# Attention scores of two heads issued in turns, with a third score tile in PSUM

## The chip, the core and the metric

The kernel runs on one core of a Trainium2 chip. Five engines work from instruction streams of their own: TensorE (PE, with its weight loads shown as PEld), VectorE (DVE), ScalarE (ACT), GpSimd (POOL) and SyncE (SP, which issues the DMAs here). Matrix products land in PSUM, which on each of 128 partitions has eight banks of 512 fp32 values. The metric is the time of one execution on the device in microseconds (us), the median of several runs.

## The reference

Input x is (4, 512, 512), batch by time by channel, and cond is (4, 512). Four layers follow each other, each added to its input:

```
x = x + attention(x, cond)        # RMS norm scaled and shifted from cond, 16 heads of 32 channels,
                                  # q and k RMS-normed, softmax over all 512 keys, o + o @ W_out
x = x + GRU(x), state0 = cond     # 512 steps in time, one after the other:
                                  #   r, z = sigmoid(x W_ih + b_ih + h W_hh + b_hh)   (two thirds of the columns)
                                  #   n = tanh(i_n + r * h_n);  h = (1 - z) * n + z * h
x = x + conv4(x, taps of cond)    # causal, over time, by channel
x = x + conv4(x, taps of cond) + b
```

All is fp32. The kernel writes most matrices as a sum of two f16 parts (hi and lo) and makes three products of them.

## The kernel before

**The two kinds of work.** The GRU is a chain of 512 steps, none of which can start before the one ahead of it. Everything else (attention of later rows, the gate inputs x W_ih, the two convolutions, the output) is background work, cut into blocks of 32 time steps: block i holds rows 32i to 32i+31 of all four batches, 128 rows in all. Block i must have its gate inputs in DRAM (`GD[i]`) before step 32i.

**The prologue** (up to step 0) makes keys (`KH`, `KL`) and values (`V`) for all of x, then the attention of block 0 and the first heads of block 1 by `q_.flush`, then the gate inputs of block 0 (`tail`).

**One step** of the loop (`for t in range(T)`) issues in this order:

- `q_.head`: background stages on DVE, ACT and POOL, within budgets `DVE_B`, `ACT_B`, `POOL_B` per step;
- 64 products into `X` (r and z) and `Y` (n) at line 1227: 16 with `A` (needed first), 48 with `BT`;
- DVE transposes `X` into `TX` (line 1241), adds into `S`; ACT makes the gates `ZT` by tanh; ACT fills `X` for the next step from `G` (`seedX`); DVE transposes `Y` into `TY` (1253), a scan forms `N` (1254); ACT takes its tanh into `D` (1255) and fills `Y` for the next step (`seedY`, line 1124);
- `q_.pe`: background products on PE, chunks whose declared costs add up to at most `PE_SLOT` = 1600 ns (`SLOT0` = 2000 for the first 40 steps); I call this the step's slot;
- `keep_warm`: a product of zeros where the slot's products had under 384 columns; it goes into an `m` tile, or into the unused part of `Y`'s bank (`idle`) where both `m` tiles are taken;
- two DVE scans give `A` and `HS`, the new state (1264, 1265), and `prep` makes `BT` and `HH` of them (1130 to 1132).

Every engine takes its instructions in this order, so background work delays the chain only where an engine has not finished it when the chain's next instruction could start.

**The background queue** (`Queue`) is a planner that runs while the program is written. A task has products in chunks, each with a declared cost, then stages on other engines, in later steps. It takes buffers by name when it starts: `m` (two PSUM tiles for transposes, projections and gate inputs), `s` (two PSUM tiles for scores), `P` (four SBUF tiles for the exponentials `PX`), `PT` (four for their transposes), `O` (one PSUM tile for the attention output). Tasks are tried in order of a priority. If a block is not ready when its gate inputs are due, `q_.flush` issues all that it still needs at once.

**One head of attention** is three tasks: `S` (scores: three chunks of four products of 32 rows of q and k, one per batch, into four bands of 32 partitions of one `ps` tile, line 439; then DVE's maximum `mx` at line 446, POOL's `nb`, ACT's exponential `PX` at line 455), `TP` (four transposes of `PX`, line 301, and a copy `PT`) and `AV` (four chunks of four products with V, line 483). Head 4j+q has its 32 channels on partitions 32q to 32q+31 of q and k.

```
for b in range(B):
    nc.tensor.matmul(t[32 * b:32 * b + 32, :], s[x_][R_, j, 32 * b:32 * b + 32], k_[R_, j, b, :],
                     start=(u == 0), stop=(u == 2), skip_group_check=True)
```

PSUM's eight banks: `X`, `N`, `Y`, two `m`, two `s`, one `O`.

Of the kernel before, what the change touches and what calls it, by code (L numbers as in the profile page):

```python
# [8 lines left out]
F32 = mybir.dt.float32  # L9
# [7 lines left out]
P = 128  # L17
# [2 lines left out]
WS = 256.0  # L20
IWS = 1.0 / WS
KS_SCALE = 32.0
PE_SLOT = 1600
SC_ = 215
SLOT0, NS0 = 2000, 40
OFF2 = 120
WARM = 384
GI_T = 2
# [4 lines left out]
          TX=(130, 0), LK=(159, 1.1), S=(4, 4.8), TP=(52, 4.7), AV=(115, 2.6))  # L33
PR1 = dict(PR, ON=(305, 0), TO=(-313, 0), WO=(-28, 0), GI=(-131, 0),
           LK=(128, 0.3), S=(67, 5.1), TP=(100, 6.1), AV=(-432, 6.6))
COLS = {SC_: 192, 680: 256, 137: 64, 150: 128, 330: 128, 140: 256, 111: 256, 123: 256}
DVE_B, ACT_B, POOL_B = 1130, 1900, 3300


# [18 lines left out]
class Queue:  # L58
# [7 lines left out]
    def add(self, tasks):  # L66
        self.pending = sorted(self.pending + list(tasks), key=lambda t: t.prio)
# [60 lines left out]
    def pe(self, budget):  # L128
# [3 lines left out]
        for t in self.pending:  # L132
# [4 lines left out]
            while t.ci < len(t.chunks) and t.chunks[t.ci][0] <= left:  # L137
                c, fn = t.chunks[t.ci]
                fn()
                left -= c  # L140
                self.cols += COLS.get(c, 512)
                t.ci += 1
# [20 lines left out]
def body(ctx, tc, x, cond, W_emb, b_emb, g_norm, W_qkv, g_q, g_k, W_out, W_ih, W_hh, b_ih, b_hh, L3_b, out):  # L163
    nc = tc.nc
# [4 lines left out]
    pg = ctx.enter_context(tc.tile_pool(name="pg", bufs=1, space=PS))  # L169
    pb = ctx.enter_context(tc.tile_pool(name="pb", bufs=1, space=PS))  # L170

    X = pg.tile([P, 256], F32, name="X")
    NN = pg.tile([P, 16, 4], F32, name="N")
    Yb = pg.tile([P, 512], F32, name="Y")
    Y, idle = Yb[:, 0:128], Yb[:, 128:512]

    def pm(name):
        return pb.tile([P, 512], F32, name=name, tag="m", bufs=2)
# [47 lines left out]
    zz = cst.tile([P, 512], F16, name="zz")  # L226
# [12 lines left out]
        for _ in range(n):  # L239
            nc.tensor.matmul(X, zz[:, 0:128], zz[:, 0:256], start=True, stop=True, skip_group_check=True)  # L240

    def keep_warm(n, to=None):

        for _ in range(n):
            nc.tensor.matmul(idle if to is None else to, zz[:, 0:128], zz[:, 0:384], start=to is not None, stop=True, skip_group_check=True)

    nc.tensor.matmul(Yb, zz[:, 0:128], zz, start=True, stop=True, skip_group_check=True)
    clear()
# [50 lines left out]
    def transpose4(dst, src, js=range(4)):  # L299
        for j in js:  # L300
            nc.tensor.transpose(dst[:, 128 * j:128 * j + 128], src[:, 128 * j:128 * j + 128], ident)  # L301
# [14 lines left out]

    X1, XN_, XT_ = {}, {}, {}
    last = dict(S=[], TP=[], R=[])
    q_ = Queue(dict(m=2, s=2, O=1, P=4, PT=4, xb=3, xhl=1, QS=3, q=1, o=1, gi=1, x1=3, L=3))

    def block_tasks(i):
        first, pre_q = i == 0, i < 2
        tl = []
        s = {}

        def add(name, h=0, **k):
            pr = (PR0, PR1)[i] if i < 2 else PR
            p, dp = pr[name[:2] if name[:2] in pr else name[0]]
            t = Task(name, prio=100 * i + p + dp * h + (OFF2 if i == 2 and p < 0 else 0), **k)
            tl.append(t)  # L330
            return t
# [83 lines left out]
        if pre_q:  # L415
            R = Task(f"R{i}")
# [3 lines left out]
        else:  # L420
            R = add(f"R{i}", deps=[Q], acq=["m", "L"], chunks=[(330, rch)], stages=[[("DVE", 410, rs0), ("Pool", 4800, lambda: None)]], rel=["m", "q"], settle=2)
# [4 lines left out]
        STask = {}  # L426
# [2 lines left out]
        prev_av = None  # L429

        def sch(j, q, u):
            def f():
                if u == 0:
                    s[("s", j, q)] = pb.tile([P, 512], F32, name="ps", tag="s", bufs=2)
                t = s[("s", j, q)]
                R_ = slice(32 * q, 32 * q + 32)
                x_, k_ = (("qh", KH), ("qh", KL), ("ql", KH))[u]
                for b in range(B):
                    nc.tensor.matmul(t[32 * b:32 * b + 32, :], s[x_][R_, j, 32 * b:32 * b + 32], k_[R_, j, b, :],  # L439
                                     start=(u == 0), stop=(u == 2), skip_group_check=True)  # L440
            return f

        def smax(j, q):
            def f():
                h = 4 * j + q
                nc.vector.tensor_reduce(s["mx"][:, h:h + 1], s[("s", j, q)], AX.X, ALU.max)  # L446
                (nc.vector if first else nc.gpsimd).tensor_tensor(s["nb"][:, h:h + 1], s["mx"][:, h:h + 1], s["nrq"][:, h:h + 1], ALU.mult)  # L447
            return f
# [10 lines left out]
        def tpch(h, ps=False):  # L459
            def piece(j):  # L460
                def f():
                    if j == 0:
                        s[("pt", h)] = pb.tile([P, 512], F32, name="ptp", tag="s" if ps else "m", bufs=2)
                    transpose4(s[("pt", h)], s["PX"][h], (j,))
                return f
            return [(150, piece(j)) for j in range(4)]
# [21 lines left out]
        for j in range(4):  # L488
            for q in range(4):
                h = 4 * j + q  # L490
                STask[h] = add(f"S{i}.{h}", h, deps=[R], acq=["s", "P"], after=last["S"], chunks=[(SC_, sch(j, q, u)) for u in range(3)],
                               stages=[[("DVE", 600, smax(j, q)), ("Pool", 150, lambda: None)], [("ACT", 720, sexp(j, q))]],
                               rel=["s"], settle=int(first))
                last["S"] = [STask[h]]
                TPs[h] = add(f"TP{i}.{h}", h, deps=[STask[h]], after=last["TP"], acq=["m", "PT"], chunks=tpch(h),
                             stages=[[("ACT", 490, tps(h))]], rel=["m", "P"], settle=int(first))
                last["TP"] = [TPs[h]]
                dep = [TPs[h]] + ([prev_av] if prev_av else [])
                AVs[h] = add(f"AV{i}.{h}", h, deps=dep, chunks=[(137, avch(h, kt)) for kt in range(4)],
                             acq=["O"] if h == 0 else [], rel=["PT"])  # L500
                prev_av = AVs[h]
# [100 lines left out]
        def tail(nx, ahead):  # L602
# [8 lines left out]
            o = s["o"] = at("o", [P, D])  # L611
# [31 lines left out]
            pg = {}  # L643

            def gik(k):
                for n in "rzn":
                    if k == 0:
                        pg[n] = pm("pgn") if n == "n" else pb.tile([P, 512], F32, name="pgi" + n, tag="s", bufs=2)
                    for m, (xa, wi) in enumerate(((xh, 0), (xl, 0), (xh, 1))):
                        nc.tensor.matmul(pg[n], xa[:, k, :], WR[n][:, wi, k, :], start=(k == 0 and m == 0), stop=(k == 3 and m == 2))  # L650

# [21 lines left out]
            for g, n in enumerate("rzn"):  # L673
                gs[n] = at("gs" + n, [P, 4, P], tag=("gs", "PT", "o")[g], bufs=(1, 4, 1)[g])
                o, v = gs[n].rearrange("p q (j s) -> p q j s", j=4), pg[n].rearrange(pj, j=4, q=4)
# [16 lines left out]


    bts = [block_tasks(0), block_tasks(1)]
    need = {i: bts[i]["tasks"] for i in range(2)}

    with ExitStack() as pre_ctx:
# [77 lines left out]
        YS, PY, XN, XHL = {}, {}, {}, {}  # L775
# [3 lines left out]
            nc.scalar.activation(YS[i], XS[i], AF.Copy, scale=RS[:, i:i + 1])  # L779

        def x_t(i, tag=None):
            PY[i] = pb.tile([P, 512], F32, name="py", tag=tag, bufs=2 if tag == "s" else 1) if tag else pm("py")
            transpose4(PY[i], YS[i])

        def x_n(i, e):
# [133 lines left out]
        KV4 = {}  # L919

        def proj(v, kt, b):
            p = pb.tile([P, 512], F32, name="pkv", tag="s", bufs=2)
            XH, XL = XHL[kt]
            n = 0
            for k in range(4):
                for (xa, wi) in ((XH, 0), (XL, 0), (XH, 1)):
                    nc.tensor.matmul(p, xa[:, k, b, :], WKV[:, wi, k, v, :], start=(n == 0), stop=(n == 11))
                    n += 1
            return p
# [87 lines left out]
        for i in range(2):  # L1017
            u, g0 = bts[i], 4 + 4 * i
# [23 lines left out]
        for g in range(33):  # L1042
            p = proj(*ORDER[g]) if g < 32 else None
# [8 lines left out]
            if g < 32:  # L1052
                v, kt, b = ORDER[g]
# [18 lines left out]
    x2b = [lt(f"x2b{i}", [P, 16, 38]) for i in range(2)]  # L1072
    VC, VU, VM = lt("VC", [P, 4, 7]), lt("VU", [P, 4, 4]), lt("VM", [P, 4, 4])
    with tc.manual_schedule(engines={ENG.PE, ENG.DVE, ENG.Activation, ENG.Pool, ENG.SP}):
        ahead = [t for t in need[1] if t.name in ("S1.0", "S1.1", "S1.2")]
        late = [t for t in need[1] if t.name == "S1.3"]
        need[1] = [t for t in need[1] if t not in ahead + late]
        q_.add(need[0] + ahead)
        q_.flush(need[0] + ahead, 1700, lambda used: keep_warm(max(0, int((1050 - used) / 160))), {8: scan_constants})
        gs0 = bts[0]["tail"](bts[1], late)  # L1080
    for i in range(1, NB):
        if i > 1:
# [13 lines left out]
    f = lambda a: a.rearrange("p a k -> p (a k)")  # L1096
# [103 lines left out]
    with tc.manual_schedule(engines={ENG.PE, ENG.DVE, ENG.Activation, ENG.Pool, ENG.SP}):  # L1200
# [3 lines left out]
        for t in range(T):  # L1204
            i = t // 32
# [36 lines left out]
            S = wk.tile([P, 64], F32, name="S", tag="S", bufs=1)[:, 0:32]  # L1242
# [10 lines left out]
            nc.vector.transpose(TY.rearrange("p h j b k -> p j h k b"), Y.rearrange("p (j h k b) -> p j h k b", j=4, h=2, k=4))  # L1253
            nc.vector.tensor_tensor_scan(f(NN), f(zt[:, 0]), TY[:, 0].rearrange("p j b k -> p (j b k)"), 0.0, ALU.mult, ALU.add)  # L1254
            nc.scalar.activation(D1[:, :, 0], NN[:, :, 3], AF.Tanh, scale=0.5 * IWS)  # L1255
            nc.vector.scalar_tensor_tensor(D1[:, :, 1], zt[:, 1, :, 2], 1.0, HH, ALU.add, ALU.mult)
            if 1 < t + 1 < T:
                seedY(t + 1)
            if t == 0:
                seed_first(1, 0)  # L1260
                seed_first(1, 1)
            q_.pe(SLOT0 if t < NS0 else PE_SLOT)
            keep_warm(-(-(WARM - q_.cols) // 384), pm("warm")[:, 0:384] if q_.free["m"] else None)
            nc.vector.tensor_tensor_scan(f(An), f(d0), f(D1), 0.0, ALU.mult, ALU.add)  # L1264
            nc.vector.tensor_tensor_scan(f(HSn), f(d0), f(D1), 0.0, ALU.mult, ALU.add)  # L1265
            A, HS = An, HSn
# [32 lines left out]
```

## Time and profile before

| | us |
|---|---|
| median of 3 runs (lowest, highest) | 1883.12 (1876.41, 1889.18) |
| the profiled execution | 1878.9 |
| its span, first to last instruction | 1876.8 |
| first scan `A` (step 0) ends at | 243.6 |
| steps 0 to 31 end, and what 31 of them take | 350.6, 107.0 |
| steps 32 to 63 end, and take | 458.1, 107.5 |
| steps 64 to 447 end, and take | 1663.2, 1205.1 (3.138 a step) |
| steps 448 to 479 end, and take | 1760.9, 97.7 |
| steps 480 to 511 end, and take | 1857.5, 96.6 (3.018 a step) |

PE is busy for 88% of the span, DVE for 72%, ACT for 65% and POOL for 25%. Times in the profile are from the span's start. A line of a group or a timeline names the engine, the source line, the operation and output<-inputs; "idle before" is the time that its engine waited just before it, with what ended the wait, and "issue" stands where the profile shows nothing that was waited for. Matrix products are pipelined: of a row of several, starts tell more than durations. The share of busy time is a mean over the whole span; the limits differ by stage, so the stages are read one by one.

### The profile page before, as it was taken

Reading aid. Unit: us, or ns where it says so; the run is one execution under the profiler, and the core shown is the slowest. Engines: PE = TensorE matmul, PEld = TensorE weight load, DVE = VectorE, ACT = ScalarE, POOL = GpSimd, SP = SyncE. Lnnn points to the kernel's source line nnn. Section 1 sums busy time; section 2 is a strip of 40 time slices with the busy share of each in tenths; the row PEclk is TensorE's granted clock in tenths of the full one; section 3 lists DMA queues with packets and bytes.
Section 4 is the critical chain, followed back from the end, with each engine's and each line's share of the span. In section 5 each row is a group of like instructions: output and inputs, shape, how many; then the busy total and the mean of one; then the engine's idle time right before and its main releaser. Section 6 shows DMA issues by size and latency. Waiting matters only on the chain.

```text
span 1876.8 us, 114013 instructions
## 1 busy us (share of the span) xinstructions
PE 1655.3 (88%) x48969; PEld 1173.1 (63%) x48969; DVE 1344.8 (72%) x4948; ACT 1220.1 (65%) x4685; POOL 468.6 (25%) x1496
## 2 busy tenths in 40 slices
PE   5788889999999999999999999999999998987553
PEld 2443557667676767676767666676667676765442
DVE  4784467786778777877777777878777877776664
ACT  4542466776767776767676767676676767665543
POOL 1366001222213131222222131313131222121112
PEclk9998899999999999999999999999999999999998
DMA  5652020101010102010101010010101010101000
GB/s 184 226 191 91 25 68 18 50 18 34 18 35 13 39 16 60 13 39 13 40 12 34 19 49 25 19 35 13 39 13 40 13 34 12 35 13 34 11 17 10
DMA packets 68921, 78.11 MB, mean 42 GB/s; under 512 B 6560, under 2 KB 54720, under 8 KB 67776
## 3 DMA queue, kind: packets, MB, share of 16 engines
q1 hardware_dynamic: 68416, 70.82, 12.5%
q8 instruction: 385, 6.31, 1.4%
q14 instruction: 120, 0.98, 0.2%
HBM read 44.58 MB, written 26.21 MB: 38 GB/s over the span
## 4 chain that ended last, share of the span: by engine, by line
PE 47%; DVE 24%; ACT 10%; DMA 8%; issue 6%; SPq 3%; POOL 2%; DVEq 0%; ACTq 0%; POOLq 0%
PE X L1227 21%; PE ps L439 6%; DVE TX L1241 5%; PE Y L1227 5%; PE pgi L568 5%; DMA G<-GD 5%; DVE TY L1253 4%; PE ptp L301 4%; DVE N L1254 4%; ACT D L1255 3%; DVE A L1264 2%; PE po L483 2%; ACT X L1121 2%; SPq L1093 2%; ACT Y L1124 1%
## 5 line engine op out<-in xcount | busy, mean ns | idle before, releaser
L1227 PEld LDWEIGHTS <-BT 128*8 128x8 f16 (+1 forms) x24576 | 450.2, 88 | 82.5 <-issue 19.1
L1227 PE MATMUL X<-Wlo,A 128*4 128x256 f16 x8192 | 313.1, 272 | 126.4 <-DVE A L1264 88.9
L1269 POOL TENSOR_TENSOR x2b<-x,HS 128x16 f32<-128x16 f32 x512 | 126.8, 248 | 1130.7 <-DVE HS L1265 1129.4
L1244 ACT ACTIVATE ZT<-S 128x32 f32<-128x32 f32 x512 | 134.9, 264 | 415.8 <-DVE S L1243 415.3
L1241 DVE STREAM_TRANSPOSE TX<-X 128x256 f32<-128x256 f32 x512 | 229.2, 448 | 210.0 <-PE X L1227 208.9
L1227 PE MATMUL X<-Whi,BT 128*8 128x256 f16 x8192 | 316.0, 273 | 2.7 <-issue 2.4
L1227 PEld LDWEIGHTS <-A 128*4 128x4 f16 x8192 | 151.4, 82 | 219.1 <-DVE A L1264 192.4
L1253 DVE STREAM_TRANSPOSE TY<-Y 128x128 f32<-128x128 f32 x512 | 205.2, 401 | 11.1 <-PE Y L1227 5.0
L1227 PE MATMUL Y<-Whi,BT 128*16 128x128 f16 x8192 | 209.2, 219 | 4.3 <-issue 4.0
L1227 PE MATMUL Y<-Wlo,BT 128*16 128x128 f16 x8192 | 207.9, 219 | 4.2 <-issue 3.7
L1121 ACT ACTIVATE X<-G 128x256 f32<-128x256 f32 x510 | 202.4, 397 | 1.1 <-DMA G<-GD 0.9
L455 ACT ACTIVATE PX<-ps,nb,rqs 128x512 f32<-128x512 f32 x256 | 195.1, 762 | 8.7 <-POOL nb L447 4.8
L1254 DVE TENSOR_TENSOR_SCAN N<-ZT,TY 128x64 f32<-128x64 f32 x512 | 153.3, 299 | 54.9 <-ACT ZT L1244 1.9
L446 DVE TENSOR_REDUCE mx<-ps 128x1 f32<-128x512 f32 x256 | 174.8, 683 | 16.0 <-PE ps L439 15.9
L1264 DVE TENSOR_TENSOR_SCAN A<-D,D 128x32 f16<-128x32 f32 x512 | 115.2, 225 | 94.2 <-ACT D L1255 91.5
L301 PE MATMUL ptp<-ident,PX 128*128 128x128 f32 x1024 | 173.3, 290 | 1.0 <-ACT gs L576 0.6
L1131 ACT ACTIVATE BT<-A 128x64 f16<-128x64 f16 x512 | 131.2, 256 | 52.8 <-DVE A L1264 4.6
L301 PEld LDWEIGHTS ptp<-ident,PX 128*128 128x128 f32 x1024 | 111.4, 143 | 81.7 <-issue 43.1
L475 ACT ACTIVATE PT<-ptp 128x512 f32<-128x512 f32 x248 | 143.3, 582 | 15.7 <-PE ptp L301 15.7
L1124 ACT ACTIVATE Y<-G 128x128 f32<-128x128 f32 x510 | 141.6, 278 | 1.0 <-DMA G<-GD 0.5
L483 PEld LDWEIGHTS po<-V,PT 128*32 128x32 f32 x8192 | 99.1, 112 | 62.5 <-issue 53.8
L483 PE MATMUL po<-V,PT 128*32 128x32 f32 x8192 | 131.1, 200 | 7.3 <-issue 6.5
(266 smaller groups left out, 2818.7 us busy)
## 6 DMA issues: line engine op xcount, KB each, us to landing
GD<-gs SPq DMA_DIRECT2D x45, 256.0 KB
G<-GD SPq DMA_DIRECT2D x512, 16.0 KB
G<-GD SPq DMA_DIRECT2D x512, 8.0 KB
xp<-in_x_dram SPq DMA_DIRECT2D x16, 256.0 KB
xb<-in_x_dram SPq DMA_DIRECT2D x16, 256.0 KB
xhl<-XD SPq DMA_DIRECT2D x32, 128.0 KB
out_dram<-ob SPq DMA_DIRECT2D x16, 256.0 KB
wst<-in_L_cond_W_qkv_dram SPq DMA_DIRECT2D x6, 512.0 KB
```

The source lines that it names most:

```text
L301: nc.tensor.transpose(dst[:, 128 * j:128 * j + 128], src[:, 128 * j:128 * j + 128], ident)
L446: nc.vector.tensor_reduce(s["mx"][:, h:h + 1], s[("s", j, q)], AX.X, ALU.max)
L455: nc.scalar.activation(pe_, s[("s", j, q)], AF.Exp, bias=s["nb"][:, h:h + 1], scale=s["rqs"][:, h:h + 1], accum_out=s["ls"][:, h:h + 1])
L475: nc.scalar.activation(pt_, s[("pt", h)], AF.Copy)
L483: nc.tensor.matmul(s["po"][32 * b:32 * b + 32, 32 * h:32 * h + 32], s["PT"][h][:, kt, 32 * b:32 * b + 32], V[:, 4 * b + kt, 32 * h:32 * h ...
L1121: nc.scalar.activation(X.rearrange("p (g c) -> p g c", g=2), G[(t // 4) % 2][:, t % 4, 0:2, :], AF.Copy)
L1124: nc.scalar.activation(Y, G[(t // 4) % 2][:, t % 4, 2, :], AF.Copy)
L1227: nc.tensor.matmul(dst[32 * qq:32 * qq + M, :], lhs, W[:, k, cols].rearrange("p g (j q s) -> p q g j s", j=4, q=4)[:, qq], start=False, st ...
L1241: nc.vector.transpose(TX.rearrange("p a r -> p (a r)"), X)
L1253: nc.vector.transpose(TY.rearrange("p h j b k -> p j h k b"), Y.rearrange("p (j h k b) -> p j h k b", j=4, h=2, k=4))
L1254: nc.vector.tensor_tensor_scan(f(NN), f(zt[:, 0]), TY[:, 0].rearrange("p j b k -> p (j b k)"), 0.0, ALU.mult, ALU.add)
L1264: nc.vector.tensor_tensor_scan(f(An), f(d0), f(D1), 0.0, ALU.mult, ALU.add)
```

## The change

Three things are changed together, with the constants that go with them:

- `N` no longer has a bank of its own: it takes 64 columns of `Y`'s bank that the products don't write. The bank that comes free is a third `s` tile.
- The scores of two heads with neighbouring partitions are one task, `SP`: each of its three chunks issues eight products, those of the two heads in turns, into two `ps` tiles. `SP` takes two `s` and two `P` at once and counts as done one step later (`settle=1`). Each head's `S` task keeps the maximum and the exponential. A chunk is declared at 225 ns for eight products (before: 215 ns for four).
- `keep_warm` is left out of a step in which both `m` tiles are taken. In the prologue its products go into `idle` as before.

`PE_SLOT` goes from 1600 to 1550 and `SLOT0` from 2000 to 1900.

```diff
-PE_SLOT = 1600
-SC_ = 215
-SLOT0, NS0 = 2000, 40
+PE_SLOT = 1550
+SC_ = 225
+SLOT0, NS0 = 1900, 40
...
-COLS = {SC_: 192, 680: 256, 137: 64, 150: 128, 330: 128, 140: 256, 111: 256, 123: 256}
+COLS = {SC_: 384, 680: 256, 137: 64, 150: 128, 330: 128, 140: 256, 111: 256, 123: 256}
...
-    NN = pg.tile([P, 16, 4], F32, name="N")
     Yb = pg.tile([P, 512], F32, name="Y")
-    Y, idle = Yb[:, 0:128], Yb[:, 128:512]
+    Y, NN = Yb[:, 0:128], Yb[:, 128:192].rearrange("p (a k) -> p a k", k=4)
+    idle = Yb[:, 128:512]
...
-    def keep_warm(n, to=None):
+    def keep_warm(n, to):
         for _ in range(n):
-            nc.tensor.matmul(idle if to is None else to, zz[:, 0:128], zz[:, 0:384], start=to is not None, stop=True, skip_group_check=True)
+            nc.tensor.matmul(to, zz[:, 0:128], zz[:, 0:384], start=True, stop=True, skip_group_check=True)
...
-    q_ = Queue(dict(m=2, s=2, O=1, P=4, PT=4, xb=3, xhl=1, QS=3, q=1, o=1, gi=1, x1=3, L=3))
+    q_ = Queue(dict(m=2, s=3, O=1, P=4, PT=4, xb=3, xhl=1, QS=3, q=1, o=1, gi=1, x1=3, L=3))
...
         def sch(j, q, u):
             def f():
                 if u == 0:
-                    s[("s", j, q)] = pb.tile([P, 512], F32, name="ps", tag="s", bufs=2)
-                t = s[("s", j, q)]
-                R_ = slice(32 * q, 32 * q + 32)
+                    for r in (q, q + 1):
+                        s[("s", j, r)] = pb.tile([P, 512], F32, name="ps", tag="s", bufs=3)
                 x_, k_ = (("qh", KH), ("qh", KL), ("ql", KH))[u]
                 for b in range(B):
-                    nc.tensor.matmul(t[32 * b:32 * b + 32, :], s[x_][R_, j, 32 * b:32 * b + 32], k_[R_, j, b, :],
-                                     start=(u == 0), stop=(u == 2), skip_group_check=True)
+                    for r in (q, q + 1):
+                        R_ = slice(32 * r, 32 * r + 32)
+                        nc.tensor.matmul(s[("s", j, r)][32 * b:32 * b + 32, :], s[x_][R_, j, 32 * b:32 * b + 32], k_[R_, j, b, :],
+                                         start=(u == 0), stop=(u == 2), skip_group_check=True)
...
-                STask[h] = add(f"S{i}.{h}", h, deps=[R], acq=["s", "P"], after=last["S"], chunks=[(SC_, sch(j, q, u)) for u in range(3)],
+                if q % 2 == 0:
+                    SP = add(f"SP{i}.{h}", h, deps=[R], acq=["s", "s", "P", "P"], after=last["S"], chunks=[(SC_, sch(j, q, u)) for u in range(3)], settle=1)
+                    last["S"] = [SP]
+                STask[h] = add(f"S{i}.{h}", h, deps=[SP],
                                stages=[[("DVE", 600, smax(j, q)), ("Pool", 150, lambda: None)], [("ACT", 720, sexp(j, q))]],
                                rel=["s"], settle=int(first))
-                last["S"] = [STask[h]]
...
-        ahead = [t for t in need[1] if t.name in ("S1.0", "S1.1", "S1.2")]
+        ahead = [t for t in need[1] if t.name in ("SP1.0", "S1.0", "S1.1", "SP1.2", "S1.2")]
...
-            keep_warm(-(-(WARM - q_.cols) // 384), pm("warm")[:, 0:384] if q_.free["m"] else None)
+            if q_.free["m"]:
+                keep_warm(-(-(WARM - q_.cols) // 384), pm("warm")[:, 0:384])
```

The other lines of the diff give the score tiles' tag three buffers wherever it is used.

More of the change, by code (lines that the diff above doesn't have):

```diff
@@ L462, in f @@
                     if j == 0:
-                        s[("pt", h)] = pb.tile([P, 512], F32, name="ptp", tag="s" if ps else "m", bufs=2)
+                        s[("pt", h)] = pb.tile([P, 512], F32, name="ptp", tag="s" if ps else "m", bufs=3 if ps else 2)
                     transpose4(s[("pt", h)], s["PX"][h], (j,))
@@ L647, in gik @@
                     if k == 0:
-                        pg[n] = pm("pgn") if n == "n" else pb.tile([P, 512], F32, name="pgi" + n, tag="s", bufs=2)
+                        pg[n] = pm("pgn") if n == "n" else pb.tile([P, 512], F32, name="pgi" + n, tag="s", bufs=3)
                     for m, (xa, wi) in enumerate(((xh, 0), (xl, 0), (xh, 1))):
@@ L781, in x_t @@
         def x_t(i, tag=None):
-            PY[i] = pb.tile([P, 512], F32, name="py", tag=tag, bufs=2 if tag == "s" else 1) if tag else pm("py")
+            PY[i] = pb.tile([P, 512], F32, name="py", tag=tag, bufs=3 if tag == "s" else 1) if tag else pm("py")
             transpose4(PY[i], YS[i])
@@ L921, in proj @@
         def proj(v, kt, b):
-            p = pb.tile([P, 512], F32, name="pkv", tag="s", bufs=2)
+            p = pb.tile([P, 512], F32, name="pkv", tag="s", bufs=3)
             XH, XL = XHL[kt]
@@ L1078, in body @@
         q_.add(need[0] + ahead)
-        q_.flush(need[0] + ahead, 1700, lambda used: keep_warm(max(0, int((1050 - used) / 160))), {8: scan_constants})
+        q_.flush(need[0] + ahead, 1700, lambda used: keep_warm(max(0, int((1050 - used) / 160)), idle), {8: scan_constants})
         gs0 = bts[0]["tail"](bts[1], late)
```

## The prediction

> **What bounds the kernel now.** I read the windows by stage first, because the page's 88% for PE is a mean over unlike stages. Columns: stretch, its length, then busy time and number of instructions of PE, PEld, DVE, ACT, POOL, then the granted clock, the DMA share and GB/s.
>
> ```profile
> 248.30:293.70 45.40, 41.61 (x1430) 30.12 (x1430) 31.23 (x116) 33.55 (x128) 5.30 (x24) 1.00 0.19 53
> 446.20:455.00 8.80, 8.76 (x244) 6.85 (x241) 3.07 (x11) 4.31 (x13) 0.44 (x2) 1.00 0.17 46
> 455.00:1663.20 1208.20, 1138.29 (x36478) 828.23 (x36477) 918.77 (x3527) 863.70 (x3441) 292.05 (x1049) 1.00 0.10 27
> 1237.60:1274.20 36.60, 35.28 (x1257) 24.92 (x1257) 28.53 (x108) 29.20 (x114) 6.57 (x26) 1.00 0.06 16
> 1760.90:1857.50 96.60, 56.68 (x2083) 40.41 (x2083) 63.08 (x269) 47.51 (x229) 18.50 (x57) 1.00 0.05 12
> 176.00:226.00 50.00, 45.23 (x898) 25.93 (x897) 24.70 (x54) 24.35 (x56) 7.23 (x28) 0.80 0.27 107
> ```
>
> The last 32 steps have no attention, and take 96.6/32 = 3.018 us each: that is the bare chain, a floor that cheaper scores don't touch. Against it the stages of the table lose 107.0 - 31 x 3.018 = 13.4 us (steps 0 to 31), 10.9 (32 to 63), 46.2 (64 to 447) and 1.1 (448 to 479): 71.6 us, of which a cheaper slot can win only what PE causes. With PE waiting for `A`, a step's first product starts 0.055 us after the scan. Summed over the steps, the starts are later than that by 9.7 us in steps 1 to 31, 7.5 in 32 to 63 (5.6 of them in one step, the second window) and 6.3 in 64 to 447: PE overruns cost 23.5 us, the rest is late DVE and ACT, and one more thing, read from the waits of PE (waited for: us, times, longest), a timeline row and the DMA queues:
>
> ```profile
> PE X L1227 <- DVE A L1264: 88.9, 140, 1.3
> PE Y L1227 <- issue: 7.7, 17, 1.1
> PE po L483 <- issue: 6.5, 9, 1.7
> ...
> 256.94 0.27 PE L1227 MATMUL Y<-Wlo,BT 128*16 128x128 f16 x5 [1.12 <-issue]
> ...
> q8 instruction: 385, 6.31, 1.4%
> ```
>
> PE stops amid `Y`'s products for 1.12 us with nothing to wait for. PE and PEld have 98,533 records, or 256 for each of the 385 packets of the instruction queue; numbering the records, all 35 such stops inside `X`, `Y` and `AV` lie at the same place of 256. So PE ran out of instructions. After a stop the next packet starts 1.05 to 1.7 us later, and the stop that needs it ends 2.2 to 2.8 us after that: some 3.7 us for 256 instructions, 69 a us, or 209 in a step of 3.02 us. The fourth window is the densest twelve steps: 2,514/36.6 = 68.7 a us.
>
> **Do eight products in turns cost what four do?** The trace has it where one head's last chunk meets the next head's first, which lies on other partitions:
>
> ```profile
> 199.32 0.40 PE L439 MATMUL ps<-KH,ql 32*32 32x512 f16 x4
> 199.33 0.39 PE L439 MATMUL ps<-KH,qh 32*32 32x512 f16 x4
> 199.56 0.38 PE L439 MATMUL ps<-KL,qh 32*32 32x512 f16 x4
> 199.77 0.38 PE L439 MATMUL ps<-KH,ql 32*32 32x512 f16 x4
> ```
>
> Two groups of four start 0.01 us apart, the next 0.23 later; chunks of one head are 0.21 apart. So a pair's chunk costs about 0.22 us, not 0.43, and a pair of heads three of them, 0.65 in place of 1.29.
>
> **The sum, part by part.**
>
> 1. The flush at step 62. It issued 8.6 us of declared work at once, and the step took 8.89 us. The changed program, whose order I read, has block 2 ready before: **-5.8**.
> 2. Other overruns in steps 1 to 63: 9.7 + 7.5 - 5.6 = 11.6, of which 2.3 are two instruction stops inside slots. Declared slots fall from 1,665 to 1,501 ns on average in steps 1 to 31; slots of gate inputs hold 15 products and not 16 (0.12 us less of 0.25 late), every second one of the early slots loses its scores (0.65), the flush at step 30 shrinks from 3.00 to 2.72 us. I leave 3.8 us standing: **-5.5** (-8 to -2).
> 3. Steps 64 to 447: of 6.3 us, 2.1 lie in steps where DVE is late anyway (a maximum, 0.68, and two taps, 0.39 each, before `TX`), 2.4 are stops; the rest goes: **-1.8**. Number and pairs of DVE and ACT stages hardly change (a maximum with taps in one step: 43 times, then 41), so what DVE and ACT cost stays, within 4 us either way.
> 4. The prologue, 20 heads of scores: -20 x 0.325 = -6.5; but its filling rule sees cheaper steps and issues 34 products of zeros for 12, 22 x 0.16 = +3.5; one more planner's step, +1; scores of head 3 of block 1 are ready ahead of the tail (PE 0.65 and part of a wait), -1.1: **-3.1**, between -9 (PE bound everywhere) and +5 (none of it PE's: here ACT's exponential, 0.97 with its accumulator, is on the chain in turns with PE).
> 5. The work ends some 13 steps sooner, so the loss of steps 448 to 479 goes: **-1.0**.
> 6. Products of zeros into `Y`'s bank waited for `seedY` at steps 16 and 417, and made each next step 0.16 late: **-0.3**. With both `m` taken nothing replaces them; the bare-chain stage keeps clock 1.00 with as little on PE.
> 7. `N` in `Y`'s bank. The built order shows one new wait: `seedY` now waits for the tanh that reads `N`, on ACT itself. Rows of ACT before:
>
> ```profile
> 901.14 0.18 ACT L1255 ACTIVATE D<-N 128x16 f32<-128x16 f32 x1
> 901.22 0.28 ACT L1124 ACTIVATE Y<-G 128x128 f32<-128x128 f32 x1
> 901.65 0.26 ACT L1131 ACTIVATE BT<-A 128x64 f16<-128x64 f16 x1 [0.15 <-DVE A L1264]
> ```
>
> `seedY` starts 0.08 after the tanh; waiting, it starts at the tanh's end plus 0.03 (the gap of `D` behind `ZT` at the last step), 0.14 later, and ends at 901.64. Behind it on ACT is `BT` at 901.65, then `HH` and the exponentials; PE needs `BT` only after 16 products of `X`, 0.44 us: **0** (0 to +0.14 x 510 = 71, a rival below). No row excludes it below zero by more than noise, and nothing is saved.
>
> 8. Instruction supply. The number of PE's instructions stays (98,530 before, 98,644 after, by the built programs), but slots with cheap scores hold more of them: of steps 64 to 447, 90 issue over 205 before (in ones and twos), 177 after (mean 226, in runs of 8 to 12). I count what exceeds 209 a step, with a stock of 50 carried over, chosen because before it then gives 11.5 us where the trace has some 12: after, 21.2. With 212 a step the difference is 6.5, with 217 it is 1.6. **+7** (0 to +18).
>
> [...]
>
> Sum: -5.8 - 5.5 - 1.8 - 3.1 - 1.0 - 0.3 + 0 + 7 = -10.5. From the profiled execution's own 1878.9 that is **1868 us**. The median of the runs lies 4.2 above that execution; on it the same change would read 1872.6. One per cent, 18.8 us, is about what a measurement of this kernel can tell from no change.
>
> [...] The rows: granted clock 0.80 in the prologue's attention (last window), 1.00 in every stage of the loop. [...]
>
> **Rivals.**
>
> - *The stops don't grow, and the prologue is bound by PE.* Then part 8 is 0 and part 4 is -6.5 or more: -21, **1858**. For it: overruns shrink, so a stop inside a slot finds room. Against: the densest stretches already run at 69 a us. 0.26.
> - *Instruction supply becomes the bound* (slower). Its place is the runs of dense steps; without a stock, 226/69 = 3.28 us a step where such steps now take some 3.08 with their late DVE: 0.2 x 177 = +35, less 17.5, **1897**. It decides from 0.1 us a dense step, where the gains are used up. 0.14.
> - *`seedY`'s wait reaches the chain*: 0.05 to 0.14 a step, **1885 to 1930**. It decides if `BT` or `X`'s 17th product starts later after `A`. 0.05.
> - *The change doesn't do what it says*: eight products take two passes. Slots with a pair then overrun by 0.6 us, 8 x 13 of them: +62, **1925**. The row at 199.33 speaks against it. 0.03.
>
> **Numbers.** The forecast, 1858 to 1880, has 0.52. Faster by over 1%: 0.26 (the first rival); within 1%: 0.56 (the forecast, and the mildest part of the second rival); slower by over 1%: 0.18. The range leaves out a tenth on each side: 1850, with part 4 at its best, to 1897, the second rival.
>
> **What would show it.** Chunks of eight 0.22 us apart, and half the busy time of the scores; no step over 5 us near step 62; bare-chain steps still at 3.018 (part 7); steps 64 to 447 at 3.13 to 3.17 us; PE's "issue" waits at `X`, `Y` and `po` longer in sum; step 0 reached 0 to 9 us sooner than 243.6. I am wrong if steps 64 to 447 fall to 3.10 or rise to 3.2.

## The result, and the profile after

The changed kernel takes **1888.31 us** (median of 20 runs, 1884.61 to 1896.13), the kernel before 1881.12 (20 runs, 1875.05 to 1891.2): a ratio of **1.0038, 95% interval 1.0024 to 1.0052**. It is 0.4% slower; 1868 us was forecast. The profiled execution took 1887.27 us, its span is 1885.5.

By stage, in us, from the ends of scan `A` as before. The last column is a kernel of the experiments below, three profiles of it:

| | before | after | `early_wait` |
|---|---|---|---|
| step 0 reached | 243.6 | 236.1 | 236.2, 236.7, 237.5 |
| steps 1 to 63 | 214.5 | 208.4 | 205.7, 206.6, 206.4 |
| steps 64 to 447 | 1205.1 | 1224.0 | 1207.1, 1210.7, 1210.0 |
| steps 448 to 511 | 194.3 | 197.5 | 193.5, 193.7, 193.6 |
| span | 1876.8 | 1885.5 | 1861.8, 1867.0, 1866.9 |

So 7.5 + 6.1 us were won up to step 63, and 18.9 + 3.3 lost behind it. I read the windows by stage again (columns as in the prediction: stretch, length, busy time and instructions of PE, PEld, DVE, ACT, POOL, granted clock, DMA share, GB/s):

```profile
176.00:226.00 50.00, 43.41 (x1038) 27.04 (x1037) 24.85 (x57) 25.30 (x61) 7.31 (x28) 1.00 0.27 108
444.50:1668.50 1224.00, 1094.41 (x36732) 825.10 (x36724) 918.78 (x3524) 895.92 (x3453) 296.22 (x1049) 1.00 0.10 27
1767.50:1866.10 98.60, 56.68 (x2083) 40.40 (x2083) 62.98 (x270) 49.60 (x229) 18.76 (x57) 1.00 0.05 12
```

The third row settles where the loss lies. In the last 32 steps there is no attention, and PE has the same 2083 products and the same 56.68 us of work as before; yet they take 98.6 us in place of 96.6, 3.081 a step in place of 3.018. **The bare chain itself has become 0.06 us longer.** The forecast had named this as its test of part 7. The first row shows a second thing that was not forecast: the prologue's attention runs at a granted clock of 1.00, where before had 0.80.

The timeline of DVE and ACT in one step finds the 0.06 us. Before:

```profile
1001.05 0.45 DVE L1241 STREAM_TRANSPOSE TX<-X 128x256 f32<-128x256 f32 x1
1001.54 0.20 DVE L1243 TENSOR_TENSOR S<-TX 128x32 f32<-128x32 f32 x1
1001.66 0.40 DVE L1253 STREAM_TRANSPOSE TY<-Y 128x128 f32<-128x128 f32 x1
1002.16 0.30 DVE L1254 TENSOR_TENSOR_SCAN N<-ZT,TY 128x64 f32<-128x64 f32 x1
...
1002.49 0.19 ACT L1255 ACTIVATE D<-N 128x16 f32<-128x16 f32 x1
1002.57 0.28 ACT L1124 ACTIVATE Y<-G 128x128 f32<-128x128 f32 x1
```

After (`N` now shows as `Y`, the tile that it lies in):

```profile
1003.52 0.30 DVE L1258 TENSOR_TENSOR_SCAN Y<-ZT,TY 128x64 f32<-128x64 f32 x1
...
1003.91 0.18 ACT L1259 ACTIVATE D<-Y 128x16 f32<-128x16 f32 x1
1004.13 0.28 ACT L1128 ACTIVATE Y<-G 128x128 f32<-128x128 f32 x1
```

Before, the tanh starts 0.03 us after the scan's end (1002.46 to 1002.49), after it 0.09 (1003.82 to 1003.91). By the records in ns the median over all steps is 34 before and 94 after. What differs is the tanh's waits, in the built program:

```
before  L1255 Activation D1<-N   [waits DVE]
after   L1259 Activation D1<-Y   [waits DVE, PE]
```

`N` now shares a tile with `Y`. PE's products into `Y` write none of the columns that the tanh reads, yet it waits for them, so in this program the wait goes by the tile: before, all 510 `seedY` waited for PE; after, none does, and the tanh, which comes first on ACT, does in all 512 steps. No record of work in the two traces carries more than one wait (before 12,101 carry one and 96,966 none, after 11,905 and 97,238). The first of the tanh's two, DVE's, the one that ends late, stands in a waiting instruction of its own; the tanh that follows waits for PE, whose last product into `Y` ended 1.10 us before the tanh starts (median after). The trace holds these waiting instructions: one stands ahead of the tanh in 509 of 512 steps after and in none before. By the medians it starts 32 ns after the scan's end, and the tanh starts 62 ns after it: 94 in all, 0.060 us more than before.

The waits of PE would have led astray. Columns: what waited and for whom, us in all, times, longest. After:

```profile
PE X L1231 <- ACT Y L1128: 199.9, 365, 1.9
...
PE Y L1231 <- issue: 7.1, 19, 0.8
...
PE X L1231 <- DVE A L1269: 6.3, 13, 1.4
...
PE po L485 <- issue: 4.6, 10, 0.9
```

Before, 88.9 us stood against scan `A`, 30.6 against `seedY`; now nearly all stands against `seedY`, as if the rival "`seedY`'s wait reaches the chain" had come true. It is only the one that ended last (1004.41, scan `A` 1004.36). `X`'s first product starts 0.055 us after `A` in both kernels, and `early_wait` below shows 165.3 us against `seedY` in a kernel whose bare chain is as short as before.

The score chunks are as forecast, eight products 0.22 us apart:

```profile
614.27 0.41 PE L441 MATMUL ps<-KH,qh 32*32 32x512 f16 x8
614.50 0.40 PE L441 MATMUL ps<-KL,qh 32*32 32x512 f16 x8
614.72 0.40 PE L441 MATMUL ps<-KH,ql 32*32 32x512 f16 x8
615.04 0.77 PE L301 MATMUL ptp<-ident,PX 128*128 128x128 f32 x5
```

### The profile page after: what moved, and what is told of

The parts are those of the page before. It is cut to its first block, busy times and chain, and to the rows that moved or that the text cites. A ratio compares the mean times of both kernels' runs of the same rounds, so it can differ in the third digit from the quotient of the medians.

```text
span 1885.5 us, 114172 instructions
## 1 busy us (share of the span) xinstructions
PE 1577.3 (84%) x49007; PEld 1147.8 (61%) x49007; DVE 1342.3 (71%) x4948; ACT 1253.7 (66%) x4685; POOL 473.5 (25%) x1496
## 3 DMA queue, kind: packets, MB, share of 16 engines
q1 hardware_dynamic: 68416, 70.82, 12.5%
## 4 chain that ended last, share of the span: by engine, by line
DVE 33%; PE 30%; ACT 11%; issue 6%; DMA 2%; SPq 1%; POOL 0%; DVEq 0%; POOLq 0%; ACTq 0%
PE X L1231 22%; DVE TX L1245 9%; DVE TY L1257 9%; DVE Y L1258 6%; ACT Y L1128 5%; ACT D L1259 4%; PE ps L441 2%; PE Y L1231 2%; DVE D L1260 2%; PE ptp L301 2%; DMA G<-GD 1%; DVE x L1165 1%; DVE mx L448 1%; DVE A L1269 1%; PE po L485 1%
## 5 line engine op out<-in xcount | busy, mean ns | idle before, releaser
L1258 DVE TENSOR_TENSOR_SCAN Y<-ZT,TY 128x64 f32<-128x64 f32 x512 | 153.4, 300 | 54.3 <-ACT ZT L1248 1.6
L301 PE MATMUL ptp<-ident,PX 128*128 128x128 f32 x1024 | 166.8, 286 | 6.4 <-ACT PT L477 2.3
L477 ACT ACTIVATE PT<-ptp 128x512 f32<-128x512 f32 x248 | 143.9, 584 | 10.2 <-PE ptp L301 10.1
L1259 ACT ACTIVATE D<-Y 128x16 f32<-128x16 f32 x512 | 95.2, 186 | 63.4 <-DVE D L1260 18.4
```

The lines of the kernel that those rows point to most:

```text
L477: nc.scalar.activation(pt_, s[("pt", h)], AF.Copy)
```

## The experiments

**1. The move of N alone.** The kernel before, with `N` in `Y`'s bank.

```diff
-    NN = pg.tile([P, 16, 4], F32, name="N")
     Yb = pg.tile([P, 512], F32, name="Y")
-    Y, idle = Yb[:, 0:128], Yb[:, 128:512]
+    Y, NN = Yb[:, 0:128], Yb[:, 128:192].rearrange("p (a k) -> p a k", k=4)
+    idle = Yb[:, 192:512]
...
```

> The kernel before, with one thing of the change alone: N takes 64 columns of Y's bank (the bank that comes free stays empty; products of zeros that go into Y's bank take the 320 columns that are left). The tanh of N then waits for DVE and, in the same step, for PE. Theory 1 (a second wait on the tanh costs 0.060 us a step): the tanh starts 0.093 us after the scan in place of 0.033, every step is 3.078 us or more, and the time is 1881 + 512 x 0.0605 = 1912 us. Theory 2 (a bank shared with Y is slower to read, whatever is waited for): the same 1912. Theory 3, the step of the prediction (N's move costs nothing): 1881.

Measured: 1904.84 us, ratio 1.0118 (1.0092 to 1.0145) to the kernel before at 1882.69. The tanh starts 95 ns after the scan, the last 32 steps take 98.6 us.

**2. The second wait alone.** The kernel before, `N` in its own bank, and the tanh told to wait for the last product into `Y` as well (`mm` returns its last product; that of the last call is `y_end`).

```diff
...
-            nc.scalar.activation(D1[:, :, 0], NN[:, :, 3], AF.Tanh, scale=0.5 * IWS)
+            d_ = nc.scalar.activation(D1[:, :, 0], NN[:, :, 3], AF.Tanh, scale=0.5 * IWS)
+            tc.add_manual_dep(d_.ins, y_end.ins.name, mybir.DependencyInfo(mybir.DependencyClass.Sync, mybir.DependencyReason.DATA), reason="w")
```

> The kernel before, N in its own bank, with one wait added: the tanh of N waits for the last product into Y too, which has ended some 0.9 us earlier. Theory 1 (the wait itself costs): 0.093 us from scan to tanh and 1912 us, as if N had moved. Theory 2 (the shared bank costs): 0.033 us and 1881 us. Theory 3 (a wait for something long done is free): 1881.

Measured: 1907.24 us, ratio 1.0122 (1.0089 to 1.0155); 95 ns; 98.6 us for the last 32 steps. No bank is shared here, so theory 2 falls: the wait is the cost. Both came out below the 1912 that was expected. Its rows:

```profile
1021.89 0.30 DVE L1255 TENSOR_TENSOR_SCAN N<-ZT,TY 128x64 f32<-128x64 f32 x1
...
1022.28 0.19 ACT L1256 ACTIVATE D<-N 128x16 f32<-128x16 f32 x1
```

**3. The changed kernel without the second wait.** `seedX`, which waits for PE in any case, waits for the last product into `Y`; then ACT has seen it, and the tanh waits for DVE alone (`seedX` returns its instruction, `mm` its last product as above).

```diff
...
-                seedX(t + 1)
+                tc.add_manual_dep(seedX(t + 1).ins, y_end.ins.name, mybir.DependencyInfo(mybir.DependencyClass.Sync, mybir.DependencyReason.DATA), reason="w")
```

> The changed kernel, N in Y's bank, but ACT waits for the last product into Y one instruction group earlier: the fill of X for the next step, which waits for PE anyway, waits for that product, and the tanh is left with its wait for DVE alone. Theory 1: 0.033 us from scan to tanh, bare-chain steps at 3.018, and 1888.3 - 511 x 0.0603 = 1857.5 us, 1.25% faster than the kernel before; less by what slots lose when each step has 0.06 us less room, up to 4 us: 1857 to 1862. Theory 2: 1888.

Measured: 1866.26 us, ratio **0.9921 (0.9896 to 0.9945)**. Two more groups of runs of the same kernel:

> The kernel of early_wait once more, beside the two above on one chip: 1866, ratio 0.992 to the kernel before, 0 us of half clock between 180 us and step 0.

> The kernel of early_wait beside the three above on one chip: 1866 to 1870, ratio 0.992 to 0.993.

1870.36, ratio 0.9933 (0.9910 to 0.9955), and 1871.16, 0.9933 (0.9917 to 0.9949). The tanh is back at 34 to 35 ns, the last 32 steps at 96.7 us. Its rows, and its window of the last 32 steps (columns as in the stage windows above):

```profile
1006.65 0.30 DVE L1259 TENSOR_TENSOR_SCAN Y<-ZT,TY 128x64 f32<-128x64 f32 x1
...
1006.98 0.19 ACT L1260 ACTIVATE D<-Y 128x16 f32<-128x16 f32 x1
```

```profile
1745.80:1842.50 96.70, 56.68 (x2083) 40.40 (x2083) 63.10 (x270) 49.52 (x229) 18.54 (x57) 1.00 0.05 12
```

and from its waits of PE:

```profile
PE X L1231 <- ACT Y L1128: 165.3, 265, 1.9
```

`N` still lies in `Y`'s bank and `seedY` still waits for the tanh, so neither costs anything to be seen. This version is 0.7 to 0.8% faster than the kernel before, the changed kernel 0.4% slower. By the medians the three experiments price the wait at +22 and +25 us added to the kernel before, and 17 to 22 taken from the changed one. The medians hold what the prologue does too (experiment 6); by the profiles, steps 1 to 511 alone take 1631.2 (`n_bank`), 1633.5 (`two_waits`) and 1630.0 us (after) with the wait, and 1613.8 (before) and 1606.3 to 1611.0 (`early_wait`) without it: 17 to 24 us. The bare 511 x 0.0603 = 30.8 is not reached. In steps 64 to 447 `n_bank` is 13.8 us longer than before, where 384 x 0.0605 = 23.2. That late work of other engines finds 0.06 us more room in each step is the likely reason; no run shows it by itself.

**4. Are the turns needed?** As `early_wait`, but each chunk issues four products of one head, then four of the other.

```diff
-                for b in range(B):
-                    for r in (q, q + 1):
+                for r in (q, q + 1):
+                    for b in range(B):
```

> The kernel of early_wait with the eight products of a chunk issued four of one head, then four of the other; same products, same plan. If only products issued in turns share the time: a pair's three chunks take 0.65 us more, the slots of some 100 pairs overrun by up to 0.6 us, and the time is 40 to 65 us over early_wait, 1900 to 1922. If two heads' fours overlap anyway, as neighbouring chunks of two heads did in the trace before: within 3 us of early_wait.

Measured: 1867.15 us, ratio 0.9920 (0.9894 to 0.9945); `early_wait` on the same chip 1866.26. From the first product of a pair to the next other product the median is 770 ns both with turns and without them, and 757 for the three chunks of a single head before. The second head costs 13 ns once it stands beside the first in a chunk; the order within the chunk does not matter.

**5. Instruction supply by itself.** The kernel before, with 30 (steps 448 to 479) and 50 (480 to 511) narrow products of zeros.

```diff
-            keep_warm(-(-(WARM - q_.cols) // 384), pm("warm")[:, 0:384] if q_.free["m"] else None)
+            if t < 448:
+                keep_warm(-(-(WARM - q_.cols) // 384), pm("warm")[:, 0:384] if q_.free["m"] else None)
+            else:
+                w_ = pm("warm") if q_.free["m"] else idle
+                for _ in range(30 if t < 480 else 50):
+                    nc.tensor.matmul(w_[0:16, 0:16], zz[:, 0:16], zz[:, 0:16], start=True, stop=True, skip_group_check=True)
```

> The kernel before, with narrow products of zeros (16 x 16) added where PE has room, in place of the one wide product: 30 in each of steps 448 to 479, 50 in each of steps 480 to 511. With its weight loads that makes some 190 and some 230 instructions of PE a step; PE's own work grows by 0.8 and 1.4 us at most, into some 1.6 us that are free. If PE is supplied with 69 instructions a us: 190/69 = 2.75 us is under the bare chain's 3.018, so steps 448 to 479 stay within 1 us of 97.7; 230/69 = 3.33 us is over it, so steps 480 to 511 take 106 us in place of 96.6 (103 to 109), with stops of PE at the same record of 256. If supply is hidden (part 8 is zero): both stretches stay as they were, 97.7 and 96.6.

Measured in one execution (1909.12 us), by the windows of steps 467 to 479 and 480 to 511:

```profile
1741.10:1780.30 39.20, 28.80 (x1222) 25.49 (x1217) 24.11 (x104) 19.05 (x92) 3.22 (x13) 1.00 0.09 22
1780.30:1887.70 107.40, 90.67 (x3652) 80.74 (x3652) 63.40 (x269) 47.67 (x229) 19.02 (x57) 1.00 0.05 13
```

With 188 instructions a step (PE and PEld in the first row), 13 steps take 39.3 us, 3.025 each: free. With 228 the last 32 steps take 107.4, where 106 was expected, and (3652 + 3652)/107.4 = 68.0 instructions a us. PE's own work is not the limit: steps 480, 481 and 486 hold 228 too and take 3.02 to 3.03, others up to 3.8, with stops at record 193 of 256. Steps 448 to 479 as a whole took 105.7 and not 97.7: I had left out that the first 19 of them still hold background products, and so up to some 345 instructions.

**6. What holds PE's clock in the prologue?** Four kernels change only the count of products of zeros there. The traces count 15 such products before and 37 after (the prediction had 12 and 34, and the expectations have some of the counts wrong by up to 3). `few_zeros` and `no_zeros` are `early_wait` with 6 and 0 of them (thresholds of 500 ns and none), `more_zeros` and `zeros_1700` are the kernel before with 31 and 62 (1400 and 1700). The edit of `few_zeros`:

```diff
-        q_.flush(need[0] + ahead, 1700, lambda used: keep_warm(max(0, int((1050 - used) / 160)), idle), {8: scan_constants})
+        q_.flush(need[0] + ahead, 1700, lambda used: keep_warm(max(0, int((500 - used) / 160)), idle), {8: scan_constants})
```

> The kernel of early_wait with fewer products of zeros in the attention of the prologue: 9 in place of 37, all near its start. If the prologue there is bound by PE's work (part 4): 28 x 0.16 = 4.5 us faster than early_wait, some 1862. If these products hold PE's clock up: stretches of half clock come back between 180 us and step 0 (before: 20 us in the profile, 48 and 51 in n_bank and two_waits, none in early_wait), step 0 is reached 5 to 15 us later than early_wait's 236.2, and the time is 1870 to 1880.

> The kernel before with more products of zeros in the attention of the prologue, some 19 more by a threshold of 1400 in place of 1050 ns. If they hold the clock up: no half clock between 180 us and step 0, and a time of 1873 to 1879 with a narrower spread than before's 1877 to 1890. If only their own work counts: 19 x 0.16 = 3 us slower, 1885.

> The kernel of early_wait without any product of zeros in the attention of the prologue (37 of them left out). If they hold PE's clock up: more half clock between 180 us and step 0 than early_wait's 0, step 0 reached 3 to 15 us later than 236.5, time 1872 to 1882. If two heads a task hold the clock up by themselves: no half clock there, step 0 at 231 to 236, time 1862 to 1868.

> The kernel before with products of zeros in the attention of the prologue up to 1700 ns in place of 1050, some 50 more. If they hold the clock up: less half clock than with 1400 (there 24 us in one profile, and the half of the runs under 1870), step 0 at 240 to 244, time 1868 to 1874 with most runs at one value. If their work costs more than the clock gives: 50 x 0.16 = 8 us over before, 1888.

From the profiles, by the granted clock (half clock: the stretches in which it is 0.50):

| kernel | zeros | at half clock from 179 us to step 0 | step 0 reached | time, ratio to before |
|---|---|---|---|---|
| before | 15 | 20.5 us | 243.6 | 1 |
| `n_bank`, `two_waits`, `supply` | 15 | 47.8, 51.2, 51.2 | 253.4, 255.9, 256.1 | |
| `more_zeros` | 31 | 23.9 | 248.3 | 1871.3, 0.9949 (0.9922 to 0.9976) |
| `zeros_1700` | 62 | 0 | 243.9 | 1880.9, 0.9995 (0.9972 to 1.0018) |
| after, `early_wait` three times, `serial` | 37 | 0 | 236.1 to 237.6 | |
| `slot_1350` (experiment 7) | 37 | 6.8 | 240.1 | |
| `few_zeros` | 6 | 6.8 | 236.4 | 1875.4, 0.9961 (0.9937 to 0.9986) |
| `no_zeros` | 0 | 17.1 | 238.5 | 1872.4, 0.9943 (0.9928 to 0.9958) |

The windows of 176 to 226 us of `two_waits` and of `no_zeros`, in this order:

```profile
176.00:226.00 50.00, 47.32 (x744) 25.06 (x743) 21.29 (x46) 19.53 (x45) 6.72 (x25) 0.57 0.27 107
```

```profile
176.00:226.00 50.00, 41.44 (x987) 26.70 (x985) 25.04 (x57) 25.05 (x61) 7.27 (x28) 0.83 0.27 107
```

More products of zeros go with less half clock, in the order of before (15, 31, 62) and in that of `early_wait` (37, 0). One profile of each is weak evidence, because executions with the same prologue differ: 20 to 51 us with 15 products, 0 to 6.8 with 37. The clocks of whole runs say the same: on one chip `zeros_1700` had 0.982 to 0.986 and the kernel before 0.974 to 0.981; on that chip `no_zeros` had 0.982 to 0.985 and `early_wait` 0.985 to 0.987.

The products cost their own work, though (from one to the next 0.16 us at clock 1.00 and 0.32 at half clock, in the profile of before): without half clock, `zeros_1700` reaches step 0 only at 243.9, as 47 x 0.16 = 7.5 us more work lets one expect, and `no_zeros` is within the interval of `early_wait`. Step 0 was not 5 to 15 us later in `few_zeros`, as the theory had it: 31 products fewer are 5 us less work, and 6.8 us of half clock cost no more. The total times don't rank these kernels by their prologues: `more_zeros` reaches step 0 4.4 us after `zeros_1700`, yet its steps 64 to 447 take 1200.3 us and those of `zeros_1700` 1207.0, in the same order of instructions; why is open. What the table does show is a rival of the whole change: the kernel before with 31 products of zeros, 1871.3 us, is as fast as `early_wait` in the same group of runs, 1870.36.

That two heads a task help the clock by themselves is possible (17.1 us of half clock with no zeros at all, against 20 to 51 with 15) but was not tried alone.

**7. Spreading the products.** `early_wait` with smaller slots from step 64 on.

```diff
-            q_.pe(SLOT0 if t < NS0 else PE_SLOT)
+            q_.pe(SLOT0 if t < NS0 else PE_SLOT if t < 64 else 1350)
```

> The kernel of early_wait with slots of 1350 in place of 1550 ns from step 64 on: the same products, spread over more steps, so that fewer steps hold more instructions than 209 (119 in place of 177; a sum as in part 8 gives 9.6 us of stops in place of 21.2), for two or three fuller steps where a block comes due (385 instructions at most). If instruction supply is what the cheap scores cost in steps 64 to 447: these take 5 to 10 us less than early_wait's 1207 to 1211, some 1200 to 1204, and the time is 1859 to 1865. If late DVE and ACT work sets those steps: 1207 to 1211 again, and 1866 to 1870.

Measured: 1893.73 us, ratio 1.0051 (1.0033 to 1.0070), against 1871.16 for `early_wait` beside it. Steps 64 to 447 take 1231.5 us. It tells nothing of supply: with 1350 ns a step a block is not ready in 32 steps, and at steps 94, 126, 158 and so on the queue flushes what is left; step 94 takes 8.66 us, most others of them 5.2 to 5.9. I had counted their instructions and not their time.

## Why the prediction was wrong

**The step that failed is part 7.** It says that the built order "shows one new wait: `seedY` now waits for the tanh", prices that wait's 0.14 us and takes 0. There were two new waits. The one on `seedY` was judged rightly; it is in `early_wait` and costs nothing. The other, on the tanh, stood in the same built order and was not priced, so it entered the sum at nothing: it measured 0.060 us on the bare chain in every step, 17 to 25 us in all. Its price was to be read in the rows of before that are shown above: `S`, with one wait, starts 0.04 after `TX` ends, but `N`, which waits for DVE's `TY` and then for ACT, starts 0.10 after `TY`, though `ZT` had ended 0.02 earlier than `TY` (median 22 ns).

The other terms, by `early_wait`, which has all of the change but this wait. The sum without part 7, -10.5, stands against -16.4, -12.5 and -11.7 of the medians. That the totals are near is partly luck, as the terms show:

- *Parts 1 and 2* (flush and early overruns, -11.3): right in kind, too large; steps 1 to 63 get 8.3 us shorter (214.5 to a mean of 206.2), or 6.8 from the mean of four profiles with the order of before there (before, `supply`, `more_zeros`, `zeros_1700`). No step from 50 to 63 takes over 3.5 us. Overruns fall from 17.2 to some 7.5 and not to 3.8.
- *Parts 3 and 8* (-1.8 + 7 = +5.2 for steps 64 to 447): right in sum. The same four profiles have 1205.1, 1204.3, 1200.3 and 1207.0, `early_wait` 1207.1, 1210.7, 1210.0: +5.1 by the means, though the four differ by 6.7 among themselves. PE's waits put down to "issue" in these steps sum to 12.6, 13.1, 10.3 and 13.5 us and to 18.2, 19.0 and 18.3: +6.1, where part 8 said 7. Before and then `early_wait`, from the waits of PE in steps 64 to 447:

```profile
PE Y L1227 <- issue: 5.8, 14, 0.8
PE po L483 <- issue: 3.6, 7, 0.8
PE X L1227 <- issue: 3.2, 7, 0.7
```

```profile
PE Y L1231 <- issue: 5.4, 14, 0.8
PE X L1231 <- issue: 5.2, 14, 0.8
PE po L485 <- issue: 5.1, 11, 0.9
PE ps L441 <- issue: 2.2, 5, 0.7
```

  In the changed kernel itself the sum is 12.8, and in `n_bank`, the order of before with the wait, 7.7: in longer steps PE stops less for instructions. So the second wait hid part 8, and this is some of why the wait cost less than 31 us.
- *Part 4* (prologue, -3.1): against the profiled execution of before it measured -6 to -7.5; the sign was right, but for a reason that the sum did not have. The kernels with before's prologue lie near a line, (255.9 - 243.6)/(51.2 - 20.5) = 0.40 us for each us of half clock. Without any it would reach step 0 at some 235.4 (an estimate from these two; 243.9 - 7.5 = 236.4 by `zeros_1700`), no later than the changed kernel's 236.1. So by this estimate the gain is the clock and not the cheaper scores, and its size changes with the execution of before that is taken: 236.1 stands against 243.6 to 256.1. The prediction had read the granted clock of before there, 0.80, and put nothing for it into its sum; after has 1.00. The stretches of half clock in the profiles last 3.4, 6.8, 10.2, 23.9, 47.8 and 51.2 us.
- *Part 5* (-1.0): 194.3 to 193.6. *Part 6* (-0.3) is too small to be seen.

All terms of the loop together come to little. Steps 1 to 511 take 1613.8, 1605.3 and 1614.4 us in the three profiles with the order of before (before, `more_zeros`, `zeros_1700`), and 1606.3, 1611.0 and 1610.0 in those of `early_wait`: 1611.2 and 1609.1 by the means, with 9 us between kernels of one order. So in the loop a gain from the cheaper scores is not shown; what all its profiles win is the prologue, where the clock is the likely cause.

Of the rivals, "`seedY`'s wait reaches the chain" (1885 to 1930) holds the measured time, but by luck: its mechanism is refuted, since `early_wait` keeps that wait. The first rival, 1858, falls with the larger stops, "two passes" with the rows 0.22 apart, and "supply becomes the bound" with stops of 6 us more and not 35.

## What to carry to other kernels

When tiles are merged, list the waits of every instruction on the critical chain before and after, and price each second wait, even one for something long done; if it delays the chain, let an earlier instruction of the same engine, one that waits for that engine anyway, take it over. A releaser in a view of waits is the one that ended last, not the one that costs; the stage with nothing else in it shows the chain's own length.

## What the runs showed of the hardware

In these rows a second wait costs by the order of the two: 0.06 to 0.07 us where the late one comes first (the tanh after, 94 ns against 34; `N`, 103 against the 34 of `S`), nothing where the late one comes last (`A` waits for DVE, then for ACT, and starts 32 ns after the tanh before and 33 after, by the medians). No run turns the order of two waits round. In `supply` PE took in 68.0 instructions a us over the last 32 steps, and 188 a step in 3.025 us cost nothing. In the prologue's attention four kernels with the same order there ran 20 to 51 us at half clock, and step 0 came some 12 us later in the worst; runs of one kernel differ in the same way (granted clock 0.985 at 1877.33 us and 0.975 at 1889.95, both the kernel before), which is likely much of its spread.
